# Bilinear field pairs on one core: stores issued by ScalarE two units later, loads by SyncE

## The chip and the metric

The kernel runs on one core of one Trainium2 chip. The metric is the device time of one execution in microseconds. The time before is 756.39 us, the median of 4 runs (756.37 to 756.62).

## The reference

There are 32 fields, a batch of 1024 and an embedding of 128. For each of the 496 pairs of fields i < j there is a matrix W of 128 x 128; the result is the transformed field i times field j, element by element.

```python
v_i = inputs[:, I_IDX, :]                             # inputs: 1024 x 32 x 128
v_j = inputs[:, J_IDX, :]
transformed = jnp.einsum('bpd,ped->bpe', v_i, W)      # W: 496 x 128 x 128
return transformed * v_j                              # 1024 x 496 x 128, all float32
```

The output is 260 MB, the inputs 49 MB.

## The kernel before

**Layout.** The host hands the inputs over with the embedding first, so that a field is a tile of 128 partitions x 1024 (`x_f`, 512 KB), and the matrices in tiles of eight (`w_c`, `WL = 8`, 512 KB). The pairs q = 0 to 495 are ordered by row: first field 30, with one pair, down to field 0 with 31 pairs. All x tiles but one stay in their own buffers; `x_0` passes through the ring of `WB = 3` buffers of the w tiles.

**Units.** A pair is two units u = 2q and 2q + 1, one for each half of the batch (512 columns). One unit is a PSUM tile `po` (8 buffers). The first 15 pairs are multiplied in float32 directly (line 168). For all others the operands are split into parts: `wh`, `wl`, `wd` of a chunk of two matrices (ScalarE line 100, GpSimd lines 101 to 103), and `xh`, `xl`, `xd` of half a field (ScalarE line 115, GpSimd lines 116, 117 and 121, or VectorE line 214). TensorE then adds three products: two in `first(u)` (line 171), after which ScalarE scales the sum in PSUM (line 172), and the third in `second(u)` (line 180). VectorE multiplies by field j into the output tile (line 186). `second` runs `LAG = 3` units behind `first`.

**Output.** Four pairs, that is eight units, make a group g, and a group one output tile `ot_g` of 2 MB; there are three buffers for it (`opool`, bufs=3). A full tile is one store (line 193), issued by SyncE; the first and the last groups are stored in pieces (lines 191 and 188).

**Order.** After the first loads the order of the instructions is written out by hand: the loop over u below is the program order on each engine, and each engine's queue works in that order. A DMA stands in the queue of the engine that issues it. In the loop ScalarE issues all loads: `load_x` at the start of a row, seven rows ahead, and `load_w` at pairs that the table `w_at` gives (17 pairs ahead of the tile's first pair, and 11 ahead for tiles 55 to 57, when `x_0` has a buffer of the ring). A load must wait until its buffer has been read for the last time; a store until VectorE has written its tile; and each DMA until the DMA eight before it in the program has landed, since eight semaphores go round. The splits are taken from `todo`, one after each second unit.

Of the kernel before, what the change touches and what calls it, by code (L numbers as in the profile page):

```python
# [13 lines left out]
NQ = NF * (NF - 1) // 2  # L14
# [3 lines left out]
WL = 8  # L18
# [5 lines left out]
LAG = 3  # L24
WB = 3
WLEAD = 12
XAFTER = 54
XLEAD = 5


def _pairs():
# [5 lines left out]
def kernel(  # L37
# [22 lines left out]
    nc = tc.nc  # L60
# [12 lines left out]
    def load_x(f, n=1, pieces=1, eng=None):  # L73

        if f == 0:

            t = rpool.tile([P, WL, P], F32, tag="w", name="x_0").rearrange("p q e -> p (q e)").unsqueeze(1)
        else:
            t = xpool.tile([P, n, BT], F32, tag=f"x{f}", name=f"x_{f}")
        s = BT // pieces  # L80
        for k in range(pieces):
            (eng or nc.sync).dma_start(out=t[:, :, k * s : (k + 1) * s], in_=xt[:, f : f + n, k * s : (k + 1) * s])  # L82
        for k in range(n):
            x_sb[f + k] = t[:, k, :]

    w_raw = {}

    def load_w(c, splits=(0, WL), eng=nc.scalar):
        w_raw[c] = rpool.tile([P, WL, P], F32, tag="w", name=f"w_{c}")
        for a, b in zip(splits, splits[1:]):  # L90
            eng.dma_start(out=w_raw[c][:, a:b, :], in_=wt[c, :, a:b, :])
# [15 lines left out]
    later = []  # L107
# [21 lines left out]
    todo = []  # L129
# [5 lines left out]
    todo.sort(key=lambda t: t[1])  # L135

    load_w(0, (0, 1, WL), nc.sync)
    load_x(NF - 2, pieces=2, eng=nc.scalar)
    load_x(NF - 1, pieces=2, eng=nc.scalar)
    load_x(NF - 3)  # L140
    load_x(NF - 4)
    load_w(1, eng=nc.sync)
    for f in range(NF - 5, NF - 4 - XLEAD, -1):
        load_x(f)
    load_w(2, eng=nc.sync)


# [7 lines left out]


    ctx.enter_context(tc.manual_schedule())
    po, ots = {}, {}


    def first(u):
        q, h = divmod(u, 2)
        i, c = pairs[q][0], q // WC
        r = slice(q % WC * P, (q % WC + 1) * P)
        s = slice(h * HB, (h + 1) * HB)
        po[u] = ppool.tile([P, HB], F32, tag="po", name=f"po_{u}")
        if q < nq0:
            nc.tensor.matmul(po[u], w_raw[q // WL][:, q % WL, :], x_sb[i][:, s], start=True, stop=True)  # L168
        else:
            for t in (0, 1):  # L170
                nc.tensor.matmul(po[u], w_s[c][t][:, r], x_s[i][t][:, s], start=t == 0, stop=t == 1)  # L171
            nc.scalar.mul(po[u], po[u], 1.0 + EPS)  # L172

    def second(u):
        q, h = divmod(u, 2)
        i, j = pairs[q]
        r = slice(q % WC * P, (q % WC + 1) * P)
        s = slice(h * HB, (h + 1) * HB)
        if q >= nq0:
            nc.tensor.matmul(  # L180
                po[u], w_s[q // WC][2][:, r], x_s[i][2][:, s], start=False, stop=True, skip_group_check=True
            )
        g, k = divmod(q, OG)
        if k == 0 and h == 0:
            ots[g] = opool.tile([P, OG, BT], F32, tag="ot", name=f"ot_{g}")
        nc.vector.tensor_tensor(ots[g][:, k, s], po.pop(u), x_sb[j][:, s], ALU.mult)  # L186
        if q >= NQ - 2:
            nc.sync.dma_start(out=out[g, :, k, s], in_=ots[g][:, k, s])
        elif g == 0 or q >= NQ - OG:
            if h == 1:  # L190
                nc.sync.dma_start(out=out[g, :, k], in_=ots[g][:, k])
        elif k == OG - 1 and h == 1:
            nc.sync.dma_start(out=out[g], in_=ots[g])

    for u in range(2 * NQ + LAG):
        q = u // 2
        if u < 2 * NQ:
            i, j = pairs[q]
            if u % 2 == 0 and j == i + 1 and 0 < i - 2 - XLEAD:
                load_x(i - 2 - XLEAD, eng=nc.scalar)  # L200
            first(u)
            if u % 2 == 1 and q in w_at:
                load_w(w_at[q])
            if u == 2 * x_at + 1:
                load_x(0, eng=nc.scalar)
        if u >= LAG:
            second(u - LAG)
        if u % 2 == 1:
            ready = [t for t in todo if t[0] <= q]
            if ready:  # L210
                ready[0][2](u)
                todo.remove(ready[0])
        while later and later[0][0] <= u:
            nc.vector.tensor_tensor(*later.pop(0)[1:], ALU.subtract)  # L214
    assert not todo and not later


# [25 lines left out]
```

## Time and profile before

| what | value |
|---|---|
| profiled execution, its own time | 756.39 us |
| its span, first to last instruction | 754.6 us |
| busy: TensorE, VectorE, ScalarE, GpSimd | 707.6, 621.1, 632.1, 595.8 us |
| DMA, bytes and mean rate | 310.06 MB, 411 GB/s |
| stores of 2 MB by SyncE | 122, 12.6 us from issue to landing (median) |
| loads of w by ScalarE | 59, 512 KB each, 10.3 us |
| loads of x by ScalarE | 24 of 512 KB, 11.9 us |
| mean granted TensorE clock | 0.994 |

Busy time is the time in which an engine executes; instructions that issue DMAs are not in it. In the waits, `A <- B: total, times, longest` gives the idle time of A that an event of B ended. In a timeline row the first number is the start in us, the second the length, `xN` how many instructions are merged into it, and the bracket the idle time before it and what ended it. `SPq` and `ACTq` are the queues of SyncE and ScalarE. In the rows of windows each engine's busy time is followed by its instructions, and the last three numbers are the granted clock, the share of time that the 16 DMA engines are busy, and GB/s. That share is summed over packets, so it can pass 1.00 in a short window.

### The profile page before, as it was taken

Reading aid. Unit: us, or ns where it says so; the run is one execution under the profiler, and the core shown is the slowest. Engines: PE = TensorE matmul, PEld = TensorE weight load, DVE = VectorE, ACT = ScalarE, POOL = GpSimd, SP = SyncE. Lnnn points to the kernel's source line nnn. Section 1 sums busy time; section 2 is a strip of 40 time slices with the busy share of each in tenths; the row PEclk is TensorE's granted clock in tenths of the full one; section 3 lists DMA queues with packets and bytes.
Section 4 is the critical chain, followed back from the end, with each engine's and each line's share of the span. In section 5 each row is a group of like instructions: output and inputs, shape, how many; then the busy total and the mean of one; then the engine's idle time right before and its main releaser. Section 6 shows DMA issues by size and latency. Waiting matters only on the chain.

```text
span 754.6 us, 11212 instructions
## 1 busy us (share of the span) xinstructions
PE 707.6 (94%) x2946; PEld 546.3 (72%) x2946; DVE 621.1 (82%) x1012; ACT 632.1 (84%) x1256; POOL 595.8 (79%) x863
## 2 busy tenths in 40 slices
PE   7989999999999999999999999999999999999993
PEld 3567776767777777777777777778787777777872
DVE  4889888888787778888788888888888888898884
ACT  1389888888888898898888989898898998888992
POOL 0989998888888987978878797888887878696660
PEclk9999999999999999999999999999999999999997
DMA  9999999999999999999999999999999999999997
GB/s 353 426 426 429 427 423 430 408 415 402 421 427 409 410 414 406 426 396 427 417 406 426 416 407 411 422 408 409 425 406 407 413 407 405 423 382 426 427 416 301
DMA packets 33039, 310.06 MB, mean 411 GB/s; under 512 B 3664, under 2 KB 3792, under 8 KB 17360
## 3 DMA queue, kind: packets, MB, share of 16 engines
q1 hardware_dynamic: 20448, 264.77, 84.2%
q10 hardware_dynamic: 12528, 44.57, 15.2%
q8 instruction: 24, 0.39, 0.2%
q14 instruction: 39, 0.32, 0.1%
HBM read 49.28 MB, written 260.05 MB: 410 GB/s over the span
## 4 chain that ended last, share of the span: by engine, by line
DMA 54%; DVE 23%; PE 17%; POOL 3%; issue 1%; DVEq 0%; ACT 0%; ACTq 0%; SPq 0%; POOLq 0%
DMA out_dram<-ot 52%; DVE ot L186 22%; PE po L171 11%; PE po L180 5%; DMA x<-in_xt_dram 2%; POOL xl L116 1%; DVE xd L214 1%; POOL xd L121 1%; POOL xl L117 0%; POOL wl L101 0%; DVEq L186 0%; POOL wd L103 0%; ACT xh L115 0%; ACTq L82 0%; POOL wd L102 0%
## 5 line engine op out<-in xcount | busy, mean ns | idle before, releaser
L186 DVE TENSOR_TENSOR ot<-po,x 128x512 f32<-128x512 f32 x992 | 609.5, 682 | 118.9 <-DMA out_dram<-ot 59.6
L172 ACT ACTIVATE po<-po 128x512 f32<-128x512 f32 x962 | 548.0, 583 | 87.4 <-PE po L171 41.6
L171 PE MATMUL po<-xh,wh 128*128 128x512 f32 x962 | 382.8, 398 | 20.4 <-DVE ot L186 19.9
L171 PE MATMUL po<-xl,wl 128*128 128x512 f32 x962 | 376.8, 392 | 5.7 <-POOL wl L101 5.7
L180 PE MATMUL po<-xd,wd 128*128 128x512 f32 x962 | 375.7, 391 | 4.3 <-DVE xd L214 2.9
L171 PEld LDWEIGHTS po<-xh,wh 128*128 128x128 f32 x962 | 180.4, 188 | 85.8 <-DVE ot L186 48.3
L101 POOL TENSOR_TENSOR wl<-w,wh 128x256 fp32r<-128x256 f32 x241 | 179.8, 746 | 73.1 <-ACT wh L100 71.6
L180 PEld LDWEIGHTS po<-xd,wd 128*128 128x128 f32 x962 | 180.6, 188 | 45.2 <-ACT po L172 4.9
L171 PEld LDWEIGHTS po<-xl,wl 128*128 128x128 f32 x962 | 180.7, 188 | 44.5 <-POOL wl L101 10.2
L103 POOL TENSOR_TENSOR wd<-wl,wd 128x256 fp32r<-128x256 f32 x241 | 180.3, 748 | 20.1
L102 POOL TENSOR_SCALAR wd<-wh 128x256 fp32r<-128x256 f32 x241 | 99.8, 414 | 20.3
L100 ACT ACTIVATE wh<-w 128x256 fp32r<-128x256 f32 x241 | 99.4, 413 | 5.5 <-DMA w<-in_wt_dram 3.9
L116 POOL TENSOR_TENSOR xl<-x,xh 128x512 fp32r<-128x512 f32 x52 | 68.7, 1321 | 19.0 <-ACT xh L115 18.5
L121 POOL TENSOR_TENSOR xd<-xh,xl 128x512 fp32r<-128x512 f32 x32 | 41.3, 1292 | 2.7
L115 ACT ACTIVATE xh<-x 128x512 fp32r<-128x512 f32 x52 | 32.6, 630 | 12.4 <-DMA x<-in_xt_dram 12.3
L117 POOL TENSOR_SCALAR xl<-xl 128x512 fp32r<-128x512 f32 x52 | 32.8, 631 | 4.6
L168 PE MATMUL po<-x,w 128*128 128x512 f32 x60 | 28.4, 636 | 4.1 <-DMA x<-in_xt_dram 4.1
L168 PEld LDWEIGHTS po<-x,w 128*128 128x128 f32 x60 | 11.7, 202 | 19.9 <-issue 12.7
L214 DVE TENSOR_TENSOR xd<-xh,xl 128x512 fp32r<-128x512 f32 x20 | 14.4, 721 | 3.8 <-POOL xl L117 3.8
L115 ACT ACT_TABLE_LOAD x1 | 1.3, 1283 | 4.1 <-DMA w<-in_wt_dram 4.1
L230 POOL MEMSET const-float32-0.0<- 128x1 f32 x1 | 0.1, 98 | 0.2 <-issue 0.2
L230 POOL MEMSET const-bfloat16-1.0<- 128x1 bf16 x1 | 0.1, 102 | 0.0
(2 smaller groups left out, 0.2 us busy)
## 6 DMA issues: line engine op xcount, KB each, us to landing
out_dram<-ot SPq DMA_DIRECT2D x122, 2048.0 KB, 12.6
w<-in_wt_dram ACTq DMA_DIRECT2D x59, 512.0 KB, 10.3
x<-in_xt_dram ACTq DMA_DIRECT2D x24, 512.0 KB, 11.9
x<-in_xt_dram SPq DMA_DIRECT2D x6, 512.0 KB, 8.7
out_dram<-ot SPq DMA_DIRECT2D x6, 512.0 KB, 9.9
x<-in_xt_dram ACTq DMA_DIRECT2D x4, 256.0 KB, 5.5
w<-in_wt_dram SPq DMA_DIRECT2D x2, 512.0 KB, 8.3
out_dram<-ot SPq DMA_DIRECT2D x4, 256.0 KB, 8.9
```

Source lines behind the costliest of these rows:

```text
L100: nc.scalar.mul(h, raw, 1.0 - 2.0**-13)
L101: nc.gpsimd.tensor_tensor(l, raw, h.bitcast(F32), ALU.subtract)
L102: nc.gpsimd.tensor_scalar(d, h.bitcast(F32), EPS, 1.0, ALU.mult, ALU.mult)
L103: nc.gpsimd.tensor_tensor(d, l.bitcast(F32), d.bitcast(F32), ALU.subtract)
L115: nc.scalar.mul(h, x_sb[f][:, s], 1.0 - 2.0**-13)
L116: nc.gpsimd.tensor_tensor(l, x_sb[f][:, s], h.bitcast(F32), ALU.subtract)
L121: nc.gpsimd.tensor_tensor(d, h.bitcast(F32), l.bitcast(F32), ALU.subtract)
L168: nc.tensor.matmul(po[u], w_raw[q // WL][:, q % WL, :], x_sb[i][:, s], start=True, stop=True)
L171: nc.tensor.matmul(po[u], w_s[c][t][:, r], x_s[i][t][:, s], start=t == 0, stop=t == 1)
L172: nc.scalar.mul(po[u], po[u], 1.0 + EPS)
L180: nc.tensor.matmul(po[u], w_s[q // WC][2][:, r], x_s[i][2][:, s], start=False, stop=True, skip_group_check=True)
L186: nc.vector.tensor_tensor(ots[g][:, k, s], po.pop(u), x_sb[j][:, s], ALU.mult)
```

## The change

The engines that issue change places within the loop. Loads of w and x go to SyncE's queue, in the order in which they stand in the program. Stores go to ScalarE's queue; a store is no longer put into the program directly behind VectorE's product of unit u, but is kept in a list and put there two units later (`SLAG = 2`), which with the lag of `second` is behind ScalarE's scaling of unit u + 5. The loop runs two steps longer. The loads ahead of the loop and all computing instructions stay as they are.

```diff
+SLAG = 2
...
-    def load_w(c, splits=(0, WL), eng=nc.scalar):
+    def load_w(c, splits=(0, WL), eng=nc.sync):
...
         if q >= NQ - 2:
-            nc.sync.dma_start(out=out[g, :, k, s], in_=ots[g][:, k, s])
+            stores.append((u + SLAG, out[g, :, k, s], ots[g][:, k, s]))
         elif g == 0 or q >= NQ - OG:
             if h == 1:
-                nc.sync.dma_start(out=out[g, :, k], in_=ots[g][:, k])
+                stores.append((u + SLAG, out[g, :, k], ots[g][:, k]))
         elif k == OG - 1 and h == 1:
-            nc.sync.dma_start(out=out[g], in_=ots[g])
-
-    for u in range(2 * NQ + LAG):
+            stores.append((u + SLAG, out[g], ots[g]))
+
+    for u in range(2 * NQ + LAG + SLAG):
...
-                load_x(i - 2 - XLEAD, eng=nc.scalar)
+                load_x(i - 2 - XLEAD)
             first(u)
...
-                load_x(0, eng=nc.scalar)
-        if u >= LAG:
+                load_x(0)
+        if LAG <= u < 2 * NQ + LAG:
             second(u - LAG)
+        while stores and stores[0][0] <= u - LAG:
+            nc.scalar.dma_start(*stores.pop(0)[1:])
```

More of the change, by code (lines that the diff above doesn't have):

```diff
@@ L157 @@
     ctx.enter_context(tc.manual_schedule())
-    po, ots = {}, {}
+    po, ots, stores = {}, {}, []
     def first(u):
@@ L214 @@
             nc.vector.tensor_tensor(*later.pop(0)[1:], ALU.subtract)
-    assert not todo and not later
+    assert not todo and not later and not stores
 def kernel(**inputs):
```

## The prediction

> **What bounds the kernel now.** I read the page's slices and DMA rows first.
>
> ```profile
> DMA  9999999999999999999999999999999999999997
> GB/s 353 426 426 429 427 423 430 408 415 402 421 427 409 410 414 406 426 396 427 417 406 426 416 407 411 422 408 409 425 406 407 413 407 405 423 382 426 427 416 301
> ...
> q1 hardware_dynamic: 20448, 264.77, 84.2%
> q10 hardware_dynamic: 12528, 44.57, 15.2%
> ```
>
> The DMA engines are busy in every slice, and the two queues (q1 SyncE's, q10 ScalarE's) fill 99.4% of the span. The same 310.06 MB move after the change, so only three things can move the end: stretches in which the DMA engines have nothing to do, stretches in which they move bytes slowly, and the ends of the run. The chain of waits agrees: 54% DMA. The waits say how close the rest is:
>
> ```profile
> POOL wl L101 <- ACT wh L100: 71.6, 96, 2.1
> DVE ot L186 <- DMA out_dram<-ot: 59.6, 60, 2.0
> ```
>
> VectorE waits for a free output tile (three of 2 MB) 60 times in 124 groups; GpSimd waits for ScalarE, but nobody queues behind that for long (TensorE waits for wl 16 us in all). Next, the rate by stage (length, then PE, PEld, DVE, ACT, POOL busy, clock, DMA share, GB/s):
>
> ```profile
> 30.00:135.00 105.00, 98.22 (x410) 75.45 (x409) 92.95 (x151) 89.47 (x182) 94.20 (x131) 1.00 1.01 428
> 135.00:410.00 275.00, 259.65 (x1095) 201.94 (x1094) 224.39 (x368) 240.09 (x478) 233.30 (x335) 1.00 1.01 414
> 410.00:630.00 220.00, 214.29 (x920) 170.87 (x919) 187.24 (x309) 198.95 (x395) 179.44 (x265) 1.00 1.01 412
> ```
>
> The engines are called busy throughout, yet from 135 us they move 3.5% less per second. The clock is full. Microsecond by microsecond from 415 to 427 us a low window is followed by a high one (315, 479; 295, 516), but at 423 to 425 two stand together, 299 and 221, where the load issued at 419.51 us enters: a dip at a load's start. That shortfall is the one large term that could move either way. Third, the order of events around one store:
>
> ```profile
> 415.45 2.48 DVE L186 TENSOR_TENSOR ot<-po,x 128x512 f32<-128x512 f32 x4
> ...
> 417.53 2.50 ACT L172 ACTIVATE po<-po 128x512 f32<-128x512 f32 x4
> ...
> 417.95 0.33 SPq L193 DMA_DIRECT2D out_dram<-ot  x1
> ...
> 419.14 1.29 DVE L186 TENSOR_TENSOR ot<-po,x 128x512 f32<-128x512 f32 x2 [1.22 <-DMA out_dram<-ot]
> 419.51 0.33 ACTq L91 DMA_DIRECT2D w<-in_wt_dram  x1
> ```
>
> The group's last product ends at 417.93, SyncE issues 0.02 us later, VectorE then waits 1.22 us for a tile. The ScalarE operation that will stand ahead of the store, the scaling of the fifth unit further on, is the first of the four at 417.53: ScalarE is 0.4 us early. Last, the one place where the DMA engines ran dry:
>
> ```profile
> 670.00:671.00 1.00, 1.00 (x6) 0.84 (x5) 1.00 (x3) 0.90 (x2) 0.92 (x2) 1.00 0.74 311
> 671.00:672.00 1.00, 1.00 (x7) 0.81 (x6) 1.00 (x2) 0.90 (x3) 0.92 (x3) 1.00 0.27 115
> 672.00:673.00 1.00, 1.00 (x6) 0.84 (x5) 1.00 (x3) 1.00 (x3) 0.92 (x2) 1.00 0.70 197
> ```
>
> and the two weight loads that came late just before it, and the one that came after:
>
> ```profile
> 656.73 0.42 ACT L100 ACTIVATE wh<-w 128x256 fp32r<-128x256 f32 x1 [1.32 <-DMA w<-in_wt_dram]
> 657.98 0.33 ACTq L91 DMA_DIRECT2D w<-in_wt_dram  x1
> ...
> 668.17 0.42 ACT L100 ACTIVATE wh<-w 128x256 fp32r<-128x256 f32 x1 [1.15 <-DMA w<-in_wt_dram]
> 671.34 0.34 ACTq L91 DMA_DIRECT2D w<-in_wt_dram  x1
> ```
>
> **The change part by part.** All sums start from the profiled execution: 756.39 us with a span of 754.6, the median of the runs.
>
> *Issue cost.* ScalarE loses 83 load issues and gains 132 stores, SyncE the reverse; at 0.33 us each ScalarE's sequencer has 16 us more. It is hidden: in the lines above the load's issue lies beside a running scaling and the next operation starts 0.1 us after it. With the cover gone it would cost 16 us of an engine that is idle 122 us: 0.
>
> The Trainium skill (DMA: Bandwidth & Descriptors, section "Issuing engines are not separate DMA queues") says that DMAs of all issuers end up on the same 16 engines and interleave, so that a change of issuer saves only sequencer time. By it alone the time would stay at 756.4 us; the dip at 423 us, which comes with the order in which loads and stores are issued, is what this case has beside that rule.
>
> *The loads on SyncE.* They no longer wait for ScalarE's place in the program, only for their buffer and for the DMA eight before. A weight tile's buffer is free when GpSimd's L101 has read its last chunk. Walking the timeline, that is 2.7 to 7 us before the load's present issue almost everywhere. The late loads are those issued at 646.52 and 657.98: L101 read the last chunk of their buffers by 642.45 and 653.84, so both leave 4.1 us earlier, and the waits of 1.32 and 1.15 us go. The load issued at 671.34 needs the buffer of x_0, which L116 has read by 665.88: it leaves 5 us earlier and is there when the engines now run dry. What the dry stretch lost is 0.26 + 0.73 + 0.30 = 1.29 us at most; the neighbouring windows read over 1.00 by up to 0.07, so I take 1.1. Bounds: 0 (the stall moves) to 2.5 (both waits). **−1.1 us.** What is late next is the wait for a free output tile, as elsewhere. At the start SyncE's order becomes strict (x_23 and x_22 behind the tiles needed first), which can only help TensorE, while the DMA engines are full from 2.5 us on: 0, bounds ±0.5.
>
> *The stores on ScalarE, later.* ScalarE's sequencer stops at the store until VectorE's last product is done and its stores stand behind the fifth scaling further on. Queued behind: the next scalings, wh, xh, and so TensorE's third product and GpSimd. I compared, for all 122 stores of 2 MB, the start of that scaling with SyncE's issue: the median is 0.37 us earlier, 26 are later, by 11.9 us in all.
> Where ScalarE is early it holds: the next scaling begins 0.33 us after the store instead of 0.1, some 0.25 us for each group. ScalarE stays about five units ahead of VectorE, 3 us by 0.61 us each, and has 220 − 199 = 21 us idle over the 38 groups from 410 to 630 us, 0.55 each: hidden. Without that cover 122 × 0.25 = 30 us would be at stake.
> Where it is late the store leaves later. The trace's packet records show the first packet 1.3 us after the issue at the least (the tail), 2.5 in the median, 4 to 6 before 135 us: the difference is what stands in front, and a delay below it costs nothing. Outside the tail and the stretch of late loads, seven late stores have under 2.1 us and carry a load behind them, 0.20 to 0.50 us each, 2.24 together. Bounds 0 to 2.24; the output tiles give part of it back, since the next store has up to 0.8 us in hand. **+0.7 us.**
>
> *The tail.* From 719 us TensorE sets the pace and no load is left. The last 2 MB store leaves at 738.51 now; the scaling ahead of it starts at 738.92: 0.41 us later, with nothing queued in front. The small stores that follow wait for VectorE (end 743.67) and the DMA engines, which end at 750.1. **+0.4 us**, bounds 0.2 (the store before it) to 0.7 (plus one issue).
>
> Sum: 756.39 − 1.1 + 0.7 + 0.4 = **756.4 us**, no change. About 0.2% (1.5 us) is what a measurement of this kernel can tell from no change.
>
> **The rivals.** *Faster: the dips at the loads' starts thin out.* A load leaves at present some 1.5 us behind a store (419.51 against 417.95). From L101's ends nearly half of the loads would leave 0.4 to 0.5 us behind one, the others 1.7 to 5. Against it: dips grow as the store's first packet comes sooner, whatever the offset. For it: one load issued 0.14 us behind a store (358.42) met none. All dips gone, 135 to 630 us would run at 428: 275 × (1 − 414/428) + 220 × (1 − 412/428) = 9.0 + 8.2 = 17.2 us, but TensorE's 214 of 220 us caps the second at 5.7. Of the 14.7 a third, as not quite half of the loads move and some dips stay: 756.4 − 4.9 = 751.5 us.
>
> *Slower: ScalarE becomes the one that releases the stores.* The holds of 0.25 us add up where ScalarE has no idle time, at x splits (it is busy 1.00 in the windows of 173 to 178 us); it falls back, and stores leave behind it, not behind VectorE. It decides once ScalarE is under five units ahead at the group's end, 0.37 us from now in the median. Price: all 11.9 us of today's late stores at the worst, the 3.5 of those with under 2.4 us to their first packet at the least, without the 1.1 gained: 759.9 to 768; I take 760.
>
> *Nothing gained at 671 us*, because GpSimd's two x_0 splits (659 to 668 us) make the gap, not the late loads: 757.5, still within 0.2%.
>
> **How the numbers follow.** Faster rival 0.29; no change, the last rival with it, 0.37; slower 0.34, since the change puts a wait into a compute engine's queue and the one sure gain is 1.1 us. The forecast is the likeliest, 756.4. The range reaches to the values of both outer cases, 751.5 to 761.0 (the upper rival plus the 1.0 between its bounds and mine); the likeliest case's own is 754.9 to 757.9.
>
> **What would show it.** Right: no wait of wh for w, no dip at 671 us, wh and po starts 0.2 to 0.3 us later after each store, a store issued within 0.1 us of VectorE's last product in most groups, GB/s still near 412 from 410 us on. Wrong towards faster: that stage at 420 or more. Wrong towards slower: issues of stores 0.5 us or more behind VectorE through the middle, and TensorE waiting for L172. I would be wrong altogether if the early loads delayed the stores at the start or the DMA engines showed new empty slices.

## The result, and the profile after

The changed kernel takes 755.06 us (median of 35 runs, 754.76 to 755.81) against 756.53 for the kernel before (55 runs beside it). The ratio is 0.9981, 95% interval 0.9976 to 0.9986: 1.4 to 1.5 us faster, where no change was forecast. The profiled execution took 754.8 us with a span of 753.0.

The page of the changed kernel, slices and DMA rows (behind a queue's name stand packets, MB and the share of 16 engines):

```profile
GB/s 353 428 427 426 427 427 424 425 420 428 404 419 405 416 424 404 416 403 406 427 402 422 409 401 428 398 430 402 416 422 419 397 433 403 425 408 417 419 396 312
...
q10 hardware_dynamic: 19584, 261.10, 82.7%
q1 hardware_dynamic: 13392, 48.24, 16.7%
...
q14 instruction: 37, 0.30, 0.1%
```

and one row of the page of before that the forecast passed over:

```profile
q14 instruction: 39, 0.32, 0.1%
```

The queues have changed places, the engines are as full as before. The instructions that the profile records fell from 11212 to 10948, and with them the packets that fetch instructions from 39 to 37. That row becomes the point below.

The stages (length, then PE, PEld, DVE, ACT, POOL busy, clock, DMA share, GB/s), the waits, and the three microseconds that were dry before:

```profile
30.00:135.00 105.00, 98.62 (x407) 76.07 (x406) 92.84 (x147) 87.67 (x179) 89.38 (x125) 0.98 1.01 426
135.00:410.00 275.00, 260.09 (x1099) 202.90 (x1098) 225.63 (x371) 239.31 (x481) 234.54 (x335) 1.00 1.01 415
410.00:630.00 220.00, 214.88 (x923) 171.03 (x922) 188.85 (x308) 197.79 (x397) 180.70 (x267) 1.00 1.00 414
```

```profile
POOL wl L102 <- ACT wh L101: 71.5, 98, 3.0
DVE ot L187 <- DMA out_dram<-ot: 59.1, 67, 2.0
```

```profile
670.00:671.00 1.00, 1.00 (x6) 0.81 (x5) 0.52 (x1) 0.90 (x3) 0.83 (x3) 1.00 1.06 455
671.00:672.00 1.00, 1.00 (x6) 0.84 (x5) 1.00 (x3) 0.90 (x2) 1.00 (x2) 1.00 0.83 352
672.00:673.00 1.00, 1.00 (x7) 0.81 (x6) 1.00 (x3) 1.00 (x4) 0.83 (x3) 1.00 0.96 393
```

The rate from 135 us on is 1 to 2 GB/s higher, still far from 428. VectorE waits as long for output tiles as before. The dry stretch is gone, and so are the waits of wh for w (3.9 us in all before). The order around a store:

```profile
412.05 0.34 ACTq L210 DMA_DIRECT2D out_dram<-ot  x1
412.48 1.94 ACT L173 ACTIVATE po<-po 128x512 f32<-128x512 f32 x3
412.87 4.87 DVE L187 TENSOR_TENSOR ot<-po,x 128x512 f32<-128x512 f32 x8 [0.86 <-DMA out_dram<-ot]
413.61 0.33 SPq L92 DMA_DIRECT2D w<-in_wt_dram  x1
...
417.78 0.34 ACTq L210 DMA_DIRECT2D out_dram<-ot  x1
```

VectorE's eight products end at 417.74, ScalarE issues the store at 417.78; over all 122 stores the median distance is 0.03 us. All this is as the forecast had it, and the time is not.

### The profile page after: what moved, and what is told of

Read it like the earlier page. It is cut to its first block, busy times and chain, and to the rows that moved or that the text cites. A ratio compares the mean times of both kernels' runs of the same rounds, so it can differ in the third digit from the quotient of the medians.

```text
span 753.0 us, 10948 instructions
## 1 busy us (share of the span) xinstructions
PE 708.4 (94%) x2946; PEld 547.5 (73%) x2946; DVE 624.9 (83%) x1012; ACT 627.4 (83%) x1256; POOL 595.2 (79%) x863
## 4 chain that ended last, share of the span: by engine, by line
DMA 42%; PE 36%; DVE 9%; POOL 8%; issue 2%; ACT 2%; DVEq 0%; POOLq 0%; ACTq 0%
DMA out_dram<-ot 41%; PE po L172 22%; PE po L181 10%; DVE ot L187 8%; PE po L169 4%; POOL xd L122 2%; POOL wl L102 2%; POOL xl L117 2%; POOL wd L104 1%; ACT po L173 1%; POOL xl L118 1%; POOL wd L103 1%; ACT wh L101 1%; DVE xd L217 1%; DMA x<-in_xt_dram 0%
## 5 line engine op out<-in xcount | busy, mean ns | idle before, releaser
L187 DVE TENSOR_TENSOR ot<-po,x 128x512 f32<-128x512 f32 x992 | 610.4, 682 | 117.5 <-DMA out_dram<-ot 59.1
L102 POOL TENSOR_TENSOR wl<-w,wh 128x256 fp32r<-128x256 f32 x241 | 178.5, 741 | 72.8 <-ACT wh L101 71.5
L217 DVE TENSOR_TENSOR xd<-xh,xl 128x512 fp32r<-128x512 f32 x20 | 17.7, 886 | 0.0
## 6 DMA issues: line engine op xcount, KB each, us to landing
w<-in_wt_dram SPq DMA_DIRECT2D x61, 512.0 KB, 10.3
```

Source lines behind the costliest of these rows:

```text
L102: nc.gpsimd.tensor_tensor(l, raw, h.bitcast(F32), ALU.subtract)
```

## Which engine the time hangs on

The 4-byte receipts in the packet records, 16 for each DMA, tell when each of the 16 DMA engines has finished its part. In the kernel before one engine's receipt comes last in nearly every store: over stores 41 to 110 it is 4.8 us behind the median of the 16 (4.5 after the change), the second last 1.2 us (1.6). VectorE gets its tile when that receipt is there: in the lines around 419 us that stand in the forecast, the last receipt has arrived at 419.02 and VectorE starts at 419.14. At the end, 15 engines are done at about 749.8 us before and 749.0 after; the last receipt comes at 753.12 and 751.55. The two last receipts are 1.57 us apart, the spans 1.54. (The forecast let the DMA engines end at 750.1; one of them was at work for three microseconds more.)

This engine can be followed packet by packet, each starting where the one before ended. In the changed kernel that works for 84 of the 118 intervals between two landings, and in these there is no gap. The other 34 could not be followed, so that the engine never runs dry is shown for 84 only. Three of its intervals (own reading of the packet records; us):

```
landing to landing      its 16 KB packets                                           its 4 KB packets
 60.91 to  67.02  6.11  8 of 0.611                                                  8 of 0.159
435.68 to 440.75  5.07  0.642 0.639 0.644 0.625 0.644 0.639 0.634 0.625             none
618.48 to 623.55  5.07  0.624 0.639 0.634 0.634 0.644 0.648 0.625 0.644             none
```

From 80 to 105 us on its 16 KB packets take 0.637 us on the average, those of the other engines 0.611. 2 MB in 5.07 us are 414 GB/s, which is the rate of the middle stages; 2 MB in the 4.9 us of the other engines are 428. So the shortfall that the forecast put down to dips has the size that the pace of this one engine gives.

The Trainium skill (DMA: Bandwidth & Descriptors, section "Latency and other measured facts") says that two of the 16 engines are usually slower in traces than the others, with the rings of the software queue as its best guess at the cause. This trace has one engine that is clearly slower, its number is not recorded, and the kernel has no transfer on the software queue, so that cause can't be the one here.

Against the forecast's terms (theory A) stands theory B: only what moves this one engine's work moves the time.

## The experiments

**Half of the change alone.** Loads to SyncE with the stores left there; stores to ScalarE with the loads left there.

```diff
-    def load_w(c, splits=(0, WL), eng=nc.scalar):      # loads_sp: before, and load_x likewise
+    def load_w(c, splits=(0, WL), eng=nc.sync):
```
```diff
-            nc.sync.dma_start(out=out[g], in_=ots[g])  # stores_act: before, with the list and SLAG = 2
+            stores.append((u + SLAG, out[g], ots[g]))
```

> Half of the change alone: loads go to SyncE's queue, stores stay there too, each directly behind VectorE's product. Theory A (the late loads of tiles 55 to 57 and the dry stretch at 671 us were the loss): the loads of those tiles stand in SyncE's order behind stores of about the same time, so they leave about as in the kernel before; ratio to before 0.999 to 1.001, dry stretch still there. Theory B (one of the 16 DMA engines is behind the others and sets the time; what counts is only how much it has to move): a load waiting for its buffer holds the stores behind it, but as long as the lagging engine never runs out the time stays within 0.1% of before. Rival (loads that no longer sit in ScalarE's queue are the gain, wherever the stores are): 0.998, as after the whole change.

> The other half alone: stores on ScalarE two units later, loads stay on ScalarE at their old places. Theory A: nothing gained, the late stores cost what I had put down: +0.7 in the middle and +0.4 us in the tail, ratio 1.0015. Theory B: within 0.1% of before, unless the lower number of instructions helps; the waits of the scalings on VectorE should be fewer here too (600 in the changed kernel against 962), and if the instructions fetched are the cause the ratio is 0.998 here.

780.68 us, ratio 1.0324 (1.0308 to 1.0341), and 780.06 us, 1.0307 (1.0293 to 1.0322). Neither theory expected that. Loads on SyncE alone, page, stages and waits:

```profile
q1 hardware_dynamic: 32400, 308.30, 98.1%
```
```profile
135.00:410.00 275.00, 250.86 (x1055) 195.92 (x1054) 217.75 (x356) 231.35 (x460) 223.13 (x321) 0.99 0.99 397
410.00:630.00 220.00, 209.59 (x887) 163.45 (x885) 179.60 (x296) 193.73 (x383) 175.19 (x259) 1.00 1.00 401
```
```profile
DVE ot L186 <- DMA out_dram<-ot: 85.5, 67, 3.5
```

With loads and stores in one queue the rate falls to 397 and 401 GB/s and VectorE waits 26 us more for tiles; w loads land 13.4 us after their issue in place of 10.3. It is the same on either engine, so it is the one queue that costs 24 us, not who issues. Late issue is not the reason either: with both on SyncE each of the 122 stores still leaves 0.03 us behind VectorE's product. The gain exists only because both halves are made together. How the one queue loses the time was not pursued.

**The late loads alone.** Tiles 55 to 57 earlier, nothing else.

```diff
+        soon = {XAFTER + 1: 3, XAFTER + 2: 3, XAFTER + 3: 2}.get(c, 0)
-        w_at[max(c * WL - 3 * WC - 5 - early, free)] = c
+        w_at[max(c * WL - 3 * WC - 5 - early - soon, free)] = c
```

> The kernel before with one thing changed: the loads of w tiles 55, 56 and 57 stand 3, 3 and 2 pairs earlier in the program, still on ScalarE. Theory A: the two waits of wh for w (2.5 us) and the dry stretch at 670 to 673 us go, ratio 0.9985 (1.1 us less). Theory B: the lagging engine was at work in that stretch (it is some 4 us behind the others), so filling it brings nothing: ratio 0.9995 to 1.0005.

756.7 us, ratio 1.0003 (0.9994 to 1.0012). The windows of the dry stretch:

```profile
670.00:671.00 1.00, 1.00 (x6) 0.84 (x5) 1.00 (x3) 0.79 (x2) 0.83 (x3) 1.00 1.08 459
671.00:672.00 1.00, 1.00 (x6) 0.81 (x5) 0.68 (x2) 1.00 (x3) 1.00 (x2) 1.00 1.23 369
672.00:673.00 1.00, 1.00 (x6) 0.84 (x5) 0.99 (x2) 0.94 (x2) 0.83 (x3) 1.00 0.53 205
```

115 GB/s at 671 us have become 369, the waits of wh for w are gone, and nothing is gained: the other engines were dry, the slow one was not. In the packet records of before its packets of 16 KB follow one another without a gap from 670.71 to 673.28 us (0.656, 0.644, 0.644 and 0.639 us), while on the other 15 only two such packets start between 671.3 and 672.3.

**The late stores.** The changed kernel with the stores directly behind the product again, still on ScalarE.

```diff
-SLAG = 2
+SLAG = 0
```

> The changed kernel with the stores not two units later (SLAG 0), so that ScalarE always waits for VectorE and never the other way round. Theory A with my costs: stores late by 0.03 us only, the +0.7 and +0.4 us come back, but ScalarE holds longer, by up to 1.2 us for each group; ratio to before 0.9965 if the holds stay hidden, 1.005 if ScalarE's reserve is used up. Theory B: 0.998, like the changed kernel, while the holds are hidden.

755.03 us, ratio 0.998 (0.9971 to 0.9989): the time of the changed kernel. The place of the store in ScalarE's order costs and saves nothing. VectorE waits 33.2 us for tiles in place of 59.1, also for nothing.

**The dips at the loads' starts.** The kernel before with the w loads two pairs earlier.

```diff
-        early = 0 if XAFTER < c <= XAFTER + WB else WLEAD - 6
+        early = 0 if XAFTER < c <= XAFTER + WB else WLEAD - 4 if c <= XAFTER else WLEAD - 6
```

> The kernel before with the loads of the w tiles up to 54 put two pairs (four units) earlier into ScalarE's order, so that they leave some 1 us ahead of a store instead of 1.5 us behind one; stores stay on SyncE. If the gain of the change comes from where the loads stand relative to the stores (packets of the lagging engine are stretched less), this kernel gains most of the 1.5 us: 755.0. If it comes from what else the change brings (fewer semaphore instructions on ScalarE and two fetches fewer, or the late tiles at 650 to 670 us), no change: 756.4.

756.33 us, ratio 0.9997 (0.9988 to 1.0006). Most of the dips did go: summed over the run, the 16 KB packets that took over 0.67 us exceed 0.611 us by 13.0 us for each engine in the kernel before, by 9.4 in the changed one, by 3.2 here. The stages do not care:

```profile
135.00:410.00 275.00, 261.71 (x1097) 201.80 (x1096) 224.64 (x369) 241.12 (x480) 233.55 (x335) 1.00 1.00 414
410.00:630.00 220.00, 215.51 (x920) 170.02 (x919) 187.30 (x309) 199.26 (x395) 179.13 (x265) 1.00 1.00 413
```

**Relieving the slow engine.** Ten stores cut at partition 120, and then all full stores without the last or the first eight partitions.

```diff
-            stores.append((u + SLAG, out[g], ots[g]))
+            stores.append((u + SLAG, out[g, :120], ots[g][:120]))   # split15: and [120:], for g % 12 == 11
```

> The changed kernel with ten of its 2 MB stores (every twelfth group) cut into partitions 0 to 119 and 120 to 127. If each of the 16 DMA engines carries 8 neighbouring partitions of a store, in order, the cut takes 8 packets of 16 KB off the last engine ten times and gives one more packet to each of the first eight. Theory A (all 16 engines matter alike): about +0.3 us for the ten extra issues and receipts, 755 us. Theory B (one engine lags): if the lagging engine is the last, faster by up to its lag of about 4 us, 751 us; if it is one of the first eight, 10 x 0.61 = 6 us slower, 761 us; if it is another, no change.

> The changed kernel, but the full 2 MB stores leave out partitions 120 to 127 (16 MB of the output is not written). In the trace such a store ends with 15 receipts in place of 16: the last DMA engine has nothing to do in it. Theory B, if the slow engine is the last one: the other 15 move their packets of 16 KB in 0.611 us, a store in 4.9 us in place of 5.08, and from 105 us on nearly all of the shortfall of 24 us goes until TensorE paces: 735 to 742 us. If the slow engine is another one: no change beyond 1 us, 755 us. Theory A (the rate of all engines together counts): 6% fewer bytes of stores over 15 engines, no change, 755 us.

> As the run that leaves out partitions 120 to 127, but leaving out partitions 0 to 7. If the 120 partitions are dealt out to the first 15 engines in order, whichever they are, the last engine is spared here too, and the time is the same as there; if what is slow belongs to the partitions and not to the engine, the two runs differ.

None of the times expected came: the ten cuts cost 53 us (808.71 us, ratio 1.0695, 1.0677 to 1.0712), five us each. Without the last eight partitions the ratio is 1.0808 (1.0788 to 1.0828), with 6% fewer bytes stored; the four runs lie between 817 and 835 us. Without the first eight they lie between 785 and 809 us, too far apart to compare the two. A store of 120 partitions does end with 15 receipts, but the stage after a cut runs at 229 to 303 GB/s for some five us (97 to 102 us), at a DMA share of 0.72 to 1.15. Which engine is the slow one could not be told this way; these stores, which load the 16 engines unequally, cost more than the slow engine does. Why is open.

**Instruction packets.** The first try used empty instructions.

```diff
+        for _ in range(4):
+            nc.sync.nop(nofuse=True)      # nops_after; drains_after: nc.sync.drain()
```

> The changed kernel with four empty instructions on SyncE in every step of the loop, 3988 in all. SyncE has time to spare, so its loads are not delayed by them; what they bring is instruction fetches: 3988 x 64 bytes are about 31 packets of 8 KB, which the trace of the changed kernel shows at 0.31 us each. Theory A (the forecast's terms: dry stretch, late stores, tail): an instruction fetch is spread over or hidden, no change, 755 us. Theory B (one DMA engine that never runs dry and lags sets every store's landing, and the fetches are part of what makes it lag): up to 31 x 0.31 = 9.6 us slower, 765 us, if these fetches go to that engine; no change if they go to another one.

The profile shows the 10948 instructions and 37 packets of the changed kernel: the empty instructions did not stay in the program, and the run is a second measurement of the changed kernel (755.14 us, ratio 0.9982, 0.9973 to 0.9991).

By then the packets had been matched to the engines' instruction counts. SyncE runs 286 instructions before and 165 after. ScalarE, VectorE and GpSimd each have a packet every 128 instructions or so; the packets that none of their counts explains lie at 199.8 and 576.8 us before, at SyncE's 79th and 207th instruction, and at 290.1 us after, at its 79th. (The expectation below has 577.2 and 290.4 for the last two, since its times of packets count from a zero 0.3 to 0.4 us earlier. Its 195.7 is another packet: on the clock of the views it lies at 195.3, at VectorE's 320th instruction, in a row with its 190th and 454th, and the packets behind it are those of an engine at 0.611.) On the slow engine, before:

```
start    took   what
576.799  0.309  8 KB, instructions
577.105  0.905  16 KB of a store, 0.637 otherwise; followed on to the last receipt of that store
```

The packet at 199.8 us has the same mark (0.906 behind it). So the slow engine fetches SyncE's instructions, and the change leaves it one packet fewer (theory C). Drains, which stay in the program, test it.

> The changed kernel with four drain instructions on SyncE in every step of the loop, 3988 in all; unlike the empty instructions tried before they stay in the program. SyncE has time to spare. In the trace of before, SyncE's 128th and 256th instructions run at 347 and 717 us, and fetch packets that no other engine's count explains lie at 195.7 and 577.2 us; there the slowest DMA engine's interval between two stores is some 0.3 us longer than elsewhere. After the change one such packet is left, at 290.4 us, with the same mark. Theory B (the slowest DMA engine never runs dry, sets the time, and also fetches SyncE's instructions): 31 more packets of 8 KB, 0.31 us each, 9.6 us slower, 764 to 766 us. Theory A (fetches are hidden): no change, 755 us.

784.86 us, ratio 1.0374 (1.036 to 1.0389). The page:

```profile
span 783.3 us, 14936 instructions
...
q14 instruction: 68, 0.56, 0.2%
```

31 packets more and 784.86 − 755.06 = 29.8 us more: 0.96 us each, three times the packet's own 0.31. The records show part of the rest, since the packet behind is stretched too: at 234.906 us the fetch takes 0.332, the next 16 KB packet 0.885, and this one leads on to the last receipt of its store. By such places a fetch costs about 0.6 us; the remaining third is not in any one place. The 764 to 766 us of theory B were far too low.

> The changed kernel with 125 drains spread evenly over SyncE's order: 290 instructions there, 286 before the change, 165 after it, so that SyncE fetches two packets of 8 KB within the loop as before, in place of one. Theory C (the slowest DMA engine fetches SyncE's instructions, at 0.96 us a packet from the run with 31 more): 756.0 us, which is two thirds of the gain given back. If the fetch is the whole gain, 756.5; if the fetches are not the cause, 755.1.

> The changed kernel with one drain on SyncE in every step, 997 in all, 8 fetch packets more. Theory C: 8 x 0.96 = 7.7 us slower, 762.7 us. If it is not the packets but something that grows faster with the number (SyncE itself coming late with the loads), well under half of that.

> The kernel before with one drain on SyncE in every step, 995 in all, 8 fetch packets more: theory C expects the same price here, 7.7 us, 764.2 us, since the slowest engine sets the time in both kernels. If the price depends on SyncE's loads being late, which are not on SyncE here, no change: 756.5.

after_290 has one drain in every eighth step (`if u % 8 == 0`), the other two one in every step, in the changed kernel and in the kernel before.

| kernel | SyncE's instructions | its packets in the loop | all of q14 | time, us |
|---|---|---|---|---|
| changed | 165 | 1 | 37 | 755.06 |
| changed, stores not later (slag0) | 165 | 1 | 35 | 755.03 |
| before | 286 | 2 | 39 | 756.53 |
| before, three tiles earlier (early_tiles) | 286 | 2 | 39 | 756.7 |
| before, w loads earlier (lead2) | 286 | 2 | 39 | 756.33 |
| changed, 125 drains (after_290) | 290 | 2 | 38 | 756.28 |
| changed, 997 drains (after_1162) | 1163 | 9 | 45 | 763.12 |
| before, 995 drains (before_1281) | 1281 | 10 | 47 | 763.55 |
| changed, 3988 drains (drains_after) | 4153 | 32 | 68 | 784.86 |

The third column counts the first fetch at the 79th instruction and one more every 128. One packet more: +1.2 us; eight more: +8.1, 1.01 each; eight more in the kernel before: +7.0, 0.88 each. The run with 290 is back at the time of before, ratio 0.9995 (0.9986 to 1.0003). The price is about the same whether SyncE issues loads or stores, so it is not SyncE coming late with one of them. In the kernel before with 995 drains, all ten packets of SyncE can be found by its count (the first at its 88th instruction, the last at its 1239th), and behind each of them a 16 KB packet takes 0.89 to 0.91 us. And slag0 has two packets of ScalarE's stream fewer than the changed kernel (2084 instructions there in place of 2337) and the same time: those go to other engines.

A rival is left: packets and instructions grow together in these runs, and by the totals a price of 7 to 10 ns for each drain would fit as well. No run added instructions without adding a packet. The traces speak against it for the larger part (one execution each, only the intervals of the slow engine that can be followed): without a load and without a fetch an interval lasts 5.07 us in the changed kernel and with 125 drains, and 5.12 with 3988, where it holds some 32 drains. Over the whole run that is some 6 of the 29.8 us. An interval with a fetch is 0.55 to 0.67 us longer than others with as many load packets, in six cases. So 0.6 us of a packet's price is seen where it is fetched; the rest is not placed.

**Other streams, and the last packet.** Drains on ScalarE (one each step) and on GpSimd (one every second step); and w loads issued by GpSimd, which leaves SyncE 55 instructions and no packet in the loop.

```diff
+        nc.scalar.drain()                                     # act_drains
+        if u % 2 == 0: nc.gpsimd.drain()                      # pool_498
-                load_w(w_at[q])
+                load_w(w_at[q], eng=nc.gpsimd)                # w_pool
```

> The changed kernel with one drain on ScalarE in every step of the loop, 997 in all, which is some 8 more fetch packets of 8 KB. ScalarE has 120 us of idle time. Theory B with SyncE's fetches alone on the slowest DMA engine: no change, 755 us (757.5 if ScalarE's fetches go there too). If the time rises by more than that, the drains hold up ScalarE itself and the run says nothing.

> The changed kernel with one drain on GpSimd in every second step, 499 in all, 4 fetch packets more in GpSimd's stream. Theory C with the price on SyncE's stream alone: no change, 755.1 us, as long as GpSimd's 150 us of idle time take the drains. If any fetch costs the same: 755.1 + 3.8 = 758.9.

> The changed kernel with the loads of w within the loop issued by GpSimd in place of SyncE; stores stay on ScalarE, loads of x on SyncE. SyncE's order has 57 instructions left of 165. In the traces of before and after its first fetch within the loop comes at its 77th to 79th instruction and the next 128 or 129 later, so none should be left. Theory C: one packet fewer, 755.1 - 1.0 = 754.1 us. Against it: what GpSimd's own queue costs, which no run has shown; GpSimd reads the w tiles last and TensorE waits for it 4 us in all, so a load that holds GpSimd comes out slower than 755.1.

821.04 us (ratio 1.0858, 1.0844 to 1.0873), 776.77 us (1.0269, 1.0254 to 1.0284), 784.93 us (1.0372, 1.0356 to 1.0387). None tells anything about packets, since another engine took over. With the drains on ScalarE, GpSimd waits 143.6 us for wh (71.5 in the changed kernel). With those on GpSimd, TensorE waits 45 us for wl (4). With w loads on GpSimd its busy time rises from 595 to 630 us, and the waits read:

```profile
DVE ot L187 <- PE po L181: 72.0, 47, 11.6
...
PE po L172 <- POOL wl L102: 41.7, 24, 2.8
```

VectorE now waits for products, not for tiles. No kernel faster than the changed one came out.

## Why the prediction was wrong

**The step that failed** is the first reading: "only three things can move the end: stretches in which the DMA engines have nothing to do, stretches in which they move bytes slowly, and the ends of the run". That counts the 16 engines as one. The time is that of one of them (0.637 us for 16 KB against 0.611, which is 414 GB/s against 428), which has no idle time wherever it could be followed; what matters is how much work it has, and the sum had no term for that. The instruction packets were a row on the page, and the receipts of the single engines were in the trace.

That 755.06 us lies in the range of the likeliest case (754.9 to 757.9) is luck: of its three terms none came, and the gain of 1.4 to 1.5 us is of about the size that the forecast had called too small to tell. With this many runs it can be told: the interval is 0.05% wide to either side.

**−1.1 for the late loads**: measured 0 (early_tiles, +0.2, within its interval). The loads left early and the dry stretch closed, as forecast; but "what the dry stretch lost" was lost by engines that had time.

**+0.7 and +0.4 for the late stores and the tail**: measured 0 (slag0). The counts held: 27 of 122 stores leave late, by 10.2 us together, where 26 and 11.9 were forecast. The price did not. When a store was issued, the slow engine still needed 3.6 us or more (6 in the median) until its receipt for the store before, so a delay of 0.2 to 0.6 us put nothing back. The forecast's measure, the first packet of any engine, was too short a cover.

**Issue cost 0, holds hidden**: nothing contradicts it. ScalarE's place for the store makes no difference (slag0), and the distance of 0.03 us between product and store is the hold as described.

**What was gained instead**: SyncE's 121 instructions fewer, and with them one packet. Put back alone, they take the time to 756.28; by the two ratios that is (0.9995 − 0.9981) × 756.5 = 1.1 of the 1.4 us. The remaining 0.3 to 0.4 us lie within the intervals and are not attributed. The traces, each of one execution, point the same way but place only a part of it: at the landings of the same store with as many loads landed, the slow engine of the changed kernel gains 0.5 us on that of the kernel before across the fetch at 199.8 us, loses 0.7 across its own at 290.1, and gains 0.5 across the one at 576.8. It also gains in places where no fetch lies: it is 0.5 us behind at 105 us and 1.5 ahead at 718, so the larger part of these 2.0 us is not at the fetches.

**The rivals.** *Dips thin out*: they did, partly, and lead2 shows that nearly all of them may go without a gain; the 17.2 us were not to be had that way, as the shortfall has the size of the slow engine's 0.637 us. *ScalarE becomes the releaser*: it did not come; stores leave 0.03 us behind VectorE in the median, and the 27 late ones at most 0.6. *Nothing gained at 671 us*: right, though not for its reason; the gap closed and was worth nothing.

The Trainium skill's rule that was weighed (DMA: Bandwidth & Descriptors, section "Issuing engines are not separate DMA queues") would leave the time at 756.4. That it hardly matters which engine issues what agrees with the runs, as long as there are two; that a second issuer saves sequencer time alone does not: one queue in place of two cost 3.1 to 3.2%. And the issuer's instructions are themselves DMA traffic, here 0.9 to 1.2 us for 128 of SyncE's.

## What to carry to other kernels

Where the DMA engines read as full, look at the receipts of each engine, not at their sum: if one comes last in nearly every transfer, as here, gaps and dips of the others can be free, and that engine's work counts. Count instructions for each engine, waits included, as a source of DMA traffic; a queue moved to another engine also moves its instructions and their fetches. Test each half of a two-sided change alone: here each half lost 24 us and both together gained 1.5.

## What the runs showed of the hardware

- One of the 16 DMA engines moved 16 KB in 0.637 us from 80 to 105 us on, the others in 0.611; at the start it was as fast as they are. What slows it then was not found.
- SyncE's instructions come in packets of 8 KB for each 128, through that engine; a packet takes 0.31 us and costs 0.9 to 1.2, of which 0.6 is seen at the packet.
- The 16 KB packet behind a fetch is stretched, in the kernel before to 0.91 us behind SyncE's, to 0.96 behind VectorE's and mostly to 0.70 to 0.73 behind ScalarE's and GpSimd's, where 0.611 (0.637 on the slow engine) is usual.
- Loads of 512 KB and stores of 2 MB in one queue lost 24 us against two queues, on SyncE and on ScalarE alike.
- Ten stores of 120 + 8 partitions in place of 128 cost 53 us.
